# Counting passes tied to matmuls, tests moved into layer 1, and an earlier hub step in a two-layer graph kernel

## The chip, the cores and the metric

The kernel runs on one core of one Trainium2 chip. A core has a matmul engine (TensorE, PE in the profile, with its weight loads as PEld), a vector engine (VectorE, DVE), a scalar engine (ScalarE, ACT), GpSimd (POOL), a queue that issues plain transfers (SyncE, SP), and 16 DMA engines that serve the queues. The metric is the device time of one execution in microseconds (us), as the median of several runs.

## The reference

Two layers work on x of 2708 rows and 1024 columns, with a 2708 x 2708 matrix adj of zeros and ones, all float32.

```
layer 0:  q = x Wq^T + bq;  k = x Wk^T + bk;  v = x Wv^T + bv
          z = (q k^T / 32) * adj, where z == 0 becomes -10000
          x1 = layernorm(x + relu(softmax(z) v))
layer 1:  out = layernorm(x1 + adj (x1 W) + b)
```

adj is sparse: the chance of a one falls off with the square root of both the row's and the column's number, so that a few "hub" rows have many ones and most have few.

## The kernel before, in words

The kernel makes use of the sparseness. For each row it lists the columns that hold a one, sorts the rows by how many they have, and then gathers only the listed rows of x. Rows are worked on in 22 blocks of 128. A dense version of the whole computation stands behind it, and runs only if a flag is raised at the end: when a row has more ones than its block has slots, or when a score would make the shortcut wrong. Layer 1's output is already written by then; the flag is read last.

The stages, in the order of time:

1. **Product of M.** Since q k^T = x (Wq^T Wk) x^T, the weights are multiplied once into M (`product_of_m`, L739), as 28 half products of four steps each (`half_products`, L295; a float32 step appears as two matmuls in the profile). Alongside, rows of adj are loaded into three buffers in turn (`load_adj`), and `list_columns` (L230) lists a block: six range searches on DVE (L237), a counting pass on ACT over the same buffer (L240, a sign with a running sum), and some small DVE operations. Fourteen lists are called from here, one after every second half product. In the kernel before, the counting pass is part of `list_columns`, and an explicit dependency (`follow`) puts it behind the fourth search. It ends by asking for the next block's rows, which can be loaded when both the searches and the count are through with the buffer.
2. **y pairs.** y = x M + a constant row `y_bc` is what a row's scores are taken with. The first eight blocks (`FAMILY`) are made in four pairs (`y_pair`), each of seven half products. Before each of the first two pairs four more lists are called. Two sorts put the rows in order, one for the first eight blocks and one for the others (`sort_begin` makes classes on DVE, `sort_end` takes two small products of them on PE, at L664 and L668, and turns them into positions), and `records_out` writes the records in that order through POOL.
3. **y blocks.** The other 14 blocks of y (`y_block`, L377, 32 matmuls each). Beside them run the first attention jobs: `attend` gathers the y rows and the x rows of a block of sorted rows, takes the scores (L988), and sums x with the shares (L1045). `gather_onto` first copies `y_bc` into the buffer on ACT (L468) and then gathers y onto it with an adding transfer on POOL (L461).
4. **Layer 0's pairs.** Ten pairs of blocks, turned on PE (L907) and multiplied by Wv, then finished: bias, relu, residual, layernorm, and a scatter of x1 to memory (L894). In the last three pairs `row_constants` gathers rows of x (POOL) and multiplies each with a constant row on DVE (L1244).
5. **Layer 1.** Ten units of two blocks: gather and sum rows of x1 (`sum_rows`, L1412 and L1415), turn them, multiply by W, add the residual, layernorm, write. `test_scores` (L1255) runs ahead of it: it corrects the scores with the row constants, forms the tests, adds them over the partitions with a small product on PE (L1295), and sets the flag (L1296).

The most heavily filled rows are split over four partitions each, the "hub". `deal_hub` (L495) deals their columns out. It is a Python generator of ten steps, each called by a `next(deal)` at a chosen place. The fourth step computes places and the number `row` (L567 to L599), the fifth transposes `row` on PE (L602), the sixth to ninth gather the record and the eleven keys on POOL, and the tenth makes masks.

**What sets the order.** Each engine works through its own list in order. The lists are made when the program is built, by a scheduler that goes by priority (the order of the Python calls, and 2000 places ahead under `tc.high_priority(URGENT)`) and by its own estimate of when an operation's inputs are there. So an operation can stand earlier or later than its call: L1281 of `test_scores` runs at 319 us. `follow(later, earlier)` adds a dependency by hand, and with `same=True` one of order alone. `between[n]` holds things to be called after the n-th half product. A job list with estimated costs (`STEP`, `COST`, `credit`) decides after which step an attention job is called.

Of the kernel before, what the change touches and what calls it, by code (L numbers as in the profile page):

```python
# [9 lines left out]
F32 = mybir.dt.float32  # L10
# [11 lines left out]
P = 128  # L22
# [7 lines left out]
FAMILY = 8  # L30
# [51 lines left out]
def sparse_part(ctx, tc, x, xT, adj, wqT, wkT, wvT, bq, bk, bv, w1, b1, out):  # L82
# [28 lines left out]
    with es:  # L111
# [113 lines left out]
                    load_rows(a[:, cuts[i] + 8 * i:cuts[i + 1] + 8 * i], adj[:, cuts[i]:cuts[i + 1]], b * P, rows[b])  # L225
                loaded.append(a)

        listed = [0]

        def list_columns():  # L230
            b = listed[0]
            listed[0] += 1
            n, a = rows[b], loaded[b]

            at = lists.tile([P, RANGES, 8], U16, name="at_a", bufs=2)
            for i in range(RANGES):
                put = nc.vector.max_index(at[:n, i], ones[:n, :8], a[:n, cuts[i] + 8 * i:cuts[i + 1] + 8 * i + 8])  # L237
                if i == RANGES // 2:
                    behind = put
            put = nc.scalar.activation(junk[:n], a[:n, :AW].bitcast(U32), AF.Sign, accum_out=cnt[:n, b:b + 1])  # L240
            follow(put, behind)
            there = lists.tile([P, RANGES, 8], F32, name="there", bufs=2)
            nc.vector.tensor_tensor(there[:n], at[:n], ends[:n], op=ALU.is_lt)
            few = lists.tile([P, 8 * RANGES], F32, name="few", bufs=2)
            few3 = few.rearrange("p (i k) -> p i k", k=8)
            nc.vector.tensor_tensor(few3[:n], at[:n], base[:n], op=ALU.add)
            nc.vector.tensor_tensor(few3[:n], few3[:n], there[:n], op=ALU.mult)
            for i in range(0, KEYS, 8):
                nc.vector.max(keys[:n, b, i:i + 8], few[:n])
                if i + 8 < KEYS:  # L250
                    nc.vector.match_replace(few[:n], keys[:n, b, i:i + 8], few[:n], 0.0)
            load_adj()

        b_bc = a_bufs[2]
# [209 lines left out]
                follow(put, behind)  # L464
            return dst

        def gather_onto(what, src, at, n, dst):
            nc.scalar.copy(dst[:n], what[:n])  # L468
            return gather_at(src, at, n, dst, ALU.add)

        def gather_slot(src, at, n, dst):
# [267 lines left out]
        def product_of_m(acc, a, w, start, stop):  # L739
            nonlocal done, worked  # L740
            put = half_products(acc, a, w, start, stop)
            worked += 1
            while done < EARLY * worked // (7 * DC // 2):
                list_columns()
                done += 1
                if done == FAMILY + 1:
                    sort_begin(0)
            if not sorted_ and done > FAMILY + 2 and worked > 7 * DC // 2 - 4:
                sorted_.append(sort_end(0, put))
# [83 lines left out]

        wv_q = [None, quarters_of("wv", (1,))[0]]
        sorted_late = []
        for b in range(0, FAMILY, 2):
            while done < min(NB, EARLY + 4 * (b // 2 + 1)):
                list_columns()
                done += 1
            first = len(began)  # L840
            if b == 4:
                between[first + 6] = [lambda put: sorted_late.append(sort_end(1, put))]
            if b == 6:
                between[first + 5] = [lambda put: next(deal)]
            y_pair(b)
            if b == 0:
                records_out(*sorted_[0], 0, FAMILY, began[first + 1])
                records_back(0)
            if b == 2:
                load_last()  # L850
                sort_begin(1)
                bcast_rows(y_bc, y_col)
            if b in (0, 2):
                next(deal)
            if b >= 4:
                load_wv(range(DC // 2 + b - 4, DC // 2 + b - 2))
            if b == 4:
                records_out(*sorted_late[0], 0, NB - FAMILY)
# [28 lines left out]
            return gather_at(src, tabs[:rows[b], b, ROW:ROW + 1], rows[b], xr)  # L887

        def gather_y(b):
            return gather_onto(y_bc, y_ds[b >= FAMILY][:, :], tabs[:rows[b], b, OFF:OFF + 1], rows[b],  # L890
                               wp.tile([P, D], F32, name="yg"))

        def scatter(dst, b, n, src, group):
# [195 lines left out]
        def attend_shares(b, got):  # L1089
# [4 lines left out]
            else:  # L1094
                J, tab, far_less, rec, to, far, top = J0, tab0, less0, tab0, to_0, far_0, top2[:, 1:2]
                r = r_tile(b)
            yg = gather_onto(y_bc, y_ds[0][:, :], rec[:, OFF:OFF + 1], P, wp.tile([P, D], F32, name="yg"))
            for i, (j0, j1) in enumerate(pieces(J)):
                m = j1 - j0
                xg = [gather_slot(x, tab[:, j:j + 1], P, g_tile()) for j in range(j0, j1)]  # L1100
# [145 lines left out]

        def single_scores(b):
            n = rows[b]
            yg = gather_onto(y_bc, y_ds[b >= FAMILY][:, :], tabs[:n, b, OFF:OFF + 1], n, g_tile())
            xg = gather(x, b, 0, n)  # L1250
            s = stat.tile([P, 1], F32, name="s1")
            score(yg, xg, s[:n], n)
            masked_scores(b, 0, s[:n], less[:n, b, 0:1])

        def test_scores():  # L1255
# [35 lines left out]
            nc.vector.tensor_scalar(top2, top2, 9000.0, None, op0=ALU.is_gt)  # L1291
            nc.vector.tensor_max(some, some, top2[:, 0:1])
            nc.vector.tensor_max(some, some, top2[:, 1:2])
            mm = p_tr.tile([P, 4, P], F32, name="tr")
            nc.tensor.matmul(mm[:, 0, :1], ones, some, start=True, stop=True)  # L1295
            nc.vector.tensor_scalar(flag, mm[:1, 0, :1], 0.0, None, op0=ALU.is_gt)  # L1296

        credit = 0
# [11 lines left out]
        for i, (kind, b) in enumerate(steps):  # L1310
# [27 lines left out]
            if not left_y:  # L1338
                turn(i)
            if kind == "y":  # L1340
                if FAMILY + 1 <= b < FAMILY + 8:
                    next(deal)
                if b == FAMILY + 11:
                    records_back(1)
                    nc.sync.dma_start(out=bias_bc, in_=bv.to_broadcast([P, D]))
                (y_last if b == NB - 1 else y_block)(b)
                if b < FAMILY + 2:
                    load_wv(range(2 * (b - FAMILY), 2 * (b - FAMILY) + 2))
                if b == FAMILY + 1:
                    column_sums(NB - 1)  # L1350
                left_y -= 1
# [5 lines left out]
            elif kind == "mean":  # L1357
                rT = g_tile()[:, :DC * HUB].rearrange("p (c n) -> p c n", n=HUB)
                nc.scalar.copy(rT, xbT.unsqueeze(2).to_broadcast([P, DC, HUB]))
                po = project_mean(rT, wv_q)  # L1360
                pending = [(finish0, b_, po, gather_x(x, b_, b_ == last[-1])) for b_ in last]
            else:
                for k, b_ in enumerate(b):
                    pair_x[b_] = gather_x(x, b_, k)
                pending = [(finish_pair, b, project_pair(b, *turned[b]))]
                if i == len(steps) - 3:
                    u_bc = wp.tile([P, D], F32, name="u_bc", tag="yg")
                    bcast_rows(u_bc, u_col)
                if i >= len(steps) - 3:
                    row_constants((6, 8, 9)[i - len(steps) + 3])  # L1370
                if i == len(steps) - 2:
                    for b_ in single:
                        single_scores(b_)
                if b == pairs[0]:
                    bcast_rows(xb_bc[0], xbT)
                    spread.append(b)
# [5 lines left out]
        for p in pending:  # L1382
            p[0](*p[1:])
        assert not jobs and not c_left
        test_scores()


        xb_pool.release()
        cp = tc.alloc_tile_pool(name="c", bufs=1, side="right", reuse_waits="tile")
# [82 lines left out]
        for i, unit in enumerate(units):  # L1472
# [9 lines left out]
            if i == 4:  # L1482
                sum_rows("hub")
            pending = list(zip(unit, *work1(unit, *turned1.pop(i), xrs.pop(i))))
            if i in (4, 6):
                b = last[i // 2 - 2]
                pending.append((b, gather_x1(b), None))
# [322 lines left out]
```

## Time and profile before

The median of three runs is 1071.39 us (1070.51 to 1073.70). One execution was profiled.

| | |
|---|---|
| time of the profiled execution | 1075.12 us |
| its span, first to last instruction | 1073.4 us |
| PE busy | 960.5 us (89%) |
| DVE busy | 836.1 us (78%) |
| ACT busy | 410.8 us (38%) |
| POOL busy | 558.3 us (52%) |
| mean granted PE clock | 0.954 of full |
| bytes moved | 229 MB, 214 GB/s on average |

In time: the product of M ends at about 140 us, the y pairs at 254, the y blocks at about 454, layer 0's pairs at 744, and layer 1 goes on from 773 to the end.

A busy share says how long an engine worked, not whether anything waited for it. A wait names the engine or transfer that released it last. "Idle before" is the time that an engine stood still just before an instruction. The ends of PE's matmuls are modelled.

### The profile page before, as it was taken

Reading aid. Unit: us, or ns where it says so; the run is one execution under the profiler, and the core shown is the slowest. Engines: PE = TensorE matmul, PEld = TensorE weight load, DVE = VectorE, ACT = ScalarE, POOL = GpSimd, SP = SyncE. Lnnn points to the kernel's source line nnn. Section 1 sums busy time; section 2 is a strip of 40 time slices with the busy share of each in tenths; the row PEclk is TensorE's granted clock in tenths of the full one; section 3 lists DMA queues with packets and bytes.
Section 4 is the critical chain, followed back from the end, with each engine's and each line's share of the span. In section 5 each row is a group of like instructions: output and inputs, shape, how many; then the busy total and the mean of one; then the engine's idle time right before and its main releaser. Section 6 shows DMA issues by size and latency. Waiting matters only on the chain.

```text
span 1073.4 us, 10477 instructions
## 1 busy us (share of the span) xinstructions
PE 960.5 (89%) x2697; PEld 451.2 (42%) x2697; DVE 836.1 (78%) x2045; ACT 410.8 (38%) x917; POOL 558.3 (52%) x456
## 2 busy tenths in 40 slices
PE   7979897999949999999998989996299899989894
PEld 6434333444424444445543444442144344445341
DVE  8999998950697798958999888567859787868532
ACT  4244355542353423516343434322213333353431
POOL 0431163134668776216675663236687887758420
PEclk9998899899979999999999999999599899999998
DMA  9567767347988697327467974359797699977641
GB/s 356 165 181 244 225 193 228 118 145 240 286 276 225 177 291 210 108 60 272 136 179 225 243 217 147 130 180 368 273 275 231 213 306 289 326 217 222 205 117 42
DMA packets 103182, 229.21 MB, mean 214 GB/s; under 512 B 19775, under 2 KB 47175, under 8 KB 103113
## 3 DMA queue, kind: packets, MB, share of 16 engines
q0 software_dynamic: 51408, 159.09, 48.6%
q1 hardware_dynamic: 51704, 69.36, 19.9%
q8 instruction: 23, 0.38, 0.1%
q14 instruction: 47, 0.38, 0.1%
HBM read 218.08 MB, written 33.64 MB: 235 GB/s over the span
## 4 chain that ended last, share of the span: by engine, by line
PE 45%; DVE 15%; issue 15%; DMA 13%; POOL 8%; ACT 2%; another core or an unknown queue 0%; SPq 0%; POOLq 0%; DVEq 0%
PE po L297 29%; PE po L377 13%; DVE at_a L237 3%; POOL g L473 3%; DMA g<-in_x_dram,tabs 3%; DMA g<-x_d,tabs 2%; DVE junkv L988 2%; DVE r L1045 2%; DMA yg<-y_d,tabs 1%; DMA xr<-x_d,tabs 1%; PE tr L297 1%; DMA a<-in_adj_dram 1%; DVE part L1415 1%; DMA g<-x_d,tab 1%; PE tr L907 1%
## 5 line engine op out<-in xcount | busy, mean ns | idle before, releaser
L377 PE MATMUL po<-m,xt 128*128 128x512 f32 x416 | 181.9, 599 | 0.0
L297 PE MATMUL po<-t,s_all 128*128 128x512 f32 x320 | 147.3, 603 | 9.9 <-DVE xr L319 4.2
L988 DVE SCALAR_TENSOR_TENSOR junkv<-yg,g 128x1024 uint8<-128x1024 f32 x96 | 117.2, 1220 | 45.8 <-DMA yg<-y_d,tabs 29.7
L473 POOL DMA_INDIRECT g<-in_x_dram,tabs x77 | 101.4, 1317 | 45.4 <-issue 14.0
L377 PEld LDWEIGHTS po<-m,xt 128*128 128x128 f32 x416 | 79.6, 192 | 99.2 <-issue 98.7
L1415 DVE SCALAR_TENSOR_TENSOR r<-g,valid,r 128x1024 f32<-128x1024 f32 x77 | 98.3, 1283 | 15.0 <-DMA g<-x_d,tabs 9.5
L297 PEld LDWEIGHTS po<-t,s_all 128*128 128x128 f32 x320 | 61.0, 193 | 90.8 <-issue 72.0
L473 POOL DMA_INDIRECT g<-x_d,tabs x66 | 79.4, 1204 | 27.2 <-issue 16.4
L237 DVE FIND_INDEX8 at_a<-ones,a 128x8 uint16<-128x83 f32 (+3 forms) x132 | 83.5, 635 | 0.0
L240 ACT ACTIVATE junk<-a 128x2756 uint8<-128x2756 uint32 (+1 forms) x22 | 55.0, 2500 | 68.2 <-issue 36.4
L950 ACT ACTIVATE junks<-t,lnm 128x1024 uint8<-128x1024 f32 (+1 forms) x40 | 46.0, 1149 | 85.0 <-DVE lnm L948 83.9
L297 PE MATMUL po<-w,rT 128*128 128x512 f32 x160 | 74.3, 606 | 3.7 <-DVE t L1452 3.7
L297 PE MATMUL po<-wv,s_all 128*128 128x512 f32 x160 | 73.9, 606 | 3.0 <-DVE t L319 3.0
L1045 DVE SCALAR_TENSOR_TENSOR r<-g,pr,r 128x1024 f32<-128x1024 f32 x58 | 73.5, 1279 | 3.4 <-ACT r L1043 3.3
L297 PE MATMUL po<-wv,rT 128*128 128x512 f32 x160 | 74.4, 616 | 0.0
L297 PE MATMUL po<-t,rT 128*128 128x512 f32 x160 | 73.4, 601 | 0.5 <-DVE t L319 0.5
L297 PE MATMUL po<-w,s_all 128*128 128x512 f32 x160 | 72.3, 592 | 0.0
L963 ACT ACTIVATE t<-t,nmr,rstd 128x1024 f32<-128x1024 f32 (+1 forms) x40 | 49.1, 1238 | 59.3 <-DVE nmr L962 48.2
L908 ACT COPY rT<-tr 128x512 f32<-128x512 f32 x76 | 41.2, 589 | 78.3 <-PE tr L907 74.3
L450 ACT ACTIVATE junka<-xt 128x128 f32<-128x128 f32 x168 | 51.7, 308 | 41.8 <-PE po L297 21.9
L461 POOL DMA_INDIRECT xr<-in_x_dram,tabs x22 | 27.1, 1230 | 64.8 <-DVE t L1186 32.0
L1425 ACT COPY xr<-bias 128x1024 f32<-128x1024 f32 (+1 forms) x22 | 22.8, 1045 | 76.7 <-DVE t L1452 52.0
(414 smaller groups left out, 1742.9 us busy)
## 6 DMA issues: line engine op xcount, KB each, us to landing
xt<-in_xT_dram SPq DMA_DIRECT2D x21, 512.0 KB
y_d<-yo SPq DMA_DIRECT2D x21, 512.0 KB
a<-in_adj_dram SPq DMA_DIRECT2D x21, 413.5 KB
a<-in_adj_dram SPq DMA_DIRECT2D x21, 338.5 KB
a<-in_adj_dram SPq DMA_DIRECT2D x21, 263.5 KB
wq_i<-in_wqT_dram SPq DMA_DIRECT2D x8, 512.0 KB
wk_i<-in_wkT_dram SPq DMA_DIRECT2D x8, 512.0 KB
wv<-in_wvT_dram SPq DMA_DIRECT2D x16, 256.0 KB
```

The costliest lines, as they stand in the source:

```text
L237: put = nc.vector.max_index(at[:n, i], ones[:n, :8], a[:n, cuts[i] + 8 * i:cuts[i + 1] + 8 * i + 8])
L240: put = nc.scalar.activation(junk[:n], a[:n, :AW].bitcast(U32), AF.Sign, accum_out=cnt[:n, b:b + 1])
L297: put = nc.tensor.matmul(acc, a[:, k], w[:, k], start=start and k == 0, stop=stop and k == DC // 2 - 1, skip_group_check=True)
L377: put = nc.tensor.matmul(po, xts[b][:, c, :], m_q[c // 4][h][:, c % 4], start=(c == 0), stop=(c == DC - 1))
L450: put = nc.scalar.activation(junka[:, :xt.shape[2]], xt[:, c, :], AF.Copy, accum_out=xs[:, c, b:b + 1])
L473: nc.gpsimd.indirect_dma_start(out=dst[:n], out_offset=None, in_=src, in_offset=bass.IndirectOffsetOnAxis(ap=at, axis=0), bounds_check=N - ...
L908: nc.scalar.copy(rT[:, g * 4:g * 4 + 4, :], tr)
L950: nc.scalar.activation(junks[:n], t[:n], AF.Square, bias=nm[:n], accum_out=vs[:n])
L963: applied.append(nc.scalar.activation(t[:n], t[:n], AF.Identity, bias=nmr[:n], scale=rstd[:n]))
L988: nc.vector.scalar_tensor_tensor(junkv[:n], yg[:n], scale, xg[:n], op0=ALU.mult, op1=ALU.mult, accum_out=s)
L1045: nc.vector.scalar_tensor_tensor(r[:n], xg[j][:n], pr[:n, j:j + 1], r[:n], op0=ALU.mult, op1=ALU.add)
L1415: put = nc.vector.scalar_tensor_tensor(r[:n], xg[:n], ok[:n, j:j + 1], r[:n], op0=ALU.mult, op1=ALU.add)
```

## The change

- The counting pass leaves `list_columns` and becomes `count_columns(behind)`, which follows the half product handed to it. In the product of M a block that has been listed is counted after the next half product. In each of the first two y pairs two lists come before the pair and two after its second and fourth half products, and the counts after the first, third, fifth and seventh. The next load of adj is asked for in `count_columns`.
- `gather_onto` gets the block's number; for blocks 6 and 5 (`FIRST`) the copy of `y_bc` has the high priority.
- The hub's fourth step is called after the last y pair, and the later ones one y block earlier each.
- The four chunks of Wv that were loaded at the first two y blocks (two 256 KB halves each) are loaded one at a time at the fourth to seventh.
- The 23 row constants are taken 9, 9 and 5 in the last three pairs, before 6, 8 and 9.
- `test_scores` is called after the work of layer 1's seventh unit, and its last product and the flag (`raise_flag`) after that of the ninth, with an order behind PE's last product.

```diff
+        listed, counted = [0], [0]
 ...
-                put = nc.vector.max_index(at[:n, i], ones[:n, :8], a[:n, cuts[i] + 8 * i:cuts[i + 1] + 8 * i + 8])
-                if i == RANGES // 2:
-                    behind = put
-            put = nc.scalar.activation(junk[:n], a[:n, :AW].bitcast(U32), AF.Sign, accum_out=cnt[:n, b:b + 1])
-            follow(put, behind)
+                nc.vector.max_index(at[:n, i], ones[:n, :8], a[:n, cuts[i] + 8 * i:cuts[i + 1] + 8 * i + 8])
 ...
+        def count_columns(behind):
+            b = counted[0]
+            counted[0] += 1
+            n = rows[b]
+            put = nc.scalar.activation(junk[:n], loaded[b][:n, :AW].bitcast(U32), AF.Sign, accum_out=cnt[:n, b:b + 1])
+            follow(put, behind)
             load_adj()
 ...
-        def gather_onto(what, src, at, n, dst):
-            nc.scalar.copy(dst[:n], what[:n])
+        def gather_onto(b, what, src, at, n, dst):
+            if b in FIRST:
+                with tc.high_priority(URGENT):
+                    nc.scalar.copy(dst[:n], what[:n])
+            else:
+                nc.scalar.copy(dst[:n], what[:n])
             return gather_at(src, at, n, dst, ALU.add)
 ...
             worked += 1
+            if counted[0] < done:
+                count_columns(put)
             while done < EARLY * worked // (7 * DC // 2):
                 list_columns()
 ...
+        while counted[0] < done:
+            count_columns(began[-1])
         for b in range(0, FAMILY, 2):
-            while done < min(NB, EARLY + 4 * (b // 2 + 1)):
+            first = len(began)
+            if done < NB:
                 list_columns()
-                done += 1
-            first = len(began)
+                list_columns()
+                done += 4
+                for k in (1, 3, 5, 7):
+                    between[first + k] = [count_columns]
+                for k in (2, 4):
+                    between[first + k] = [lambda put: list_columns()]
 ...
-            if b in (0, 2):
+            if b in (0, 2, 6):
                 next(deal)
 ...
+            return some
+
+        def raise_flag(some):
             mm = p_tr.tile([P, 4, P], F32, name="tr")
-            nc.tensor.matmul(mm[:, 0, :1], ones, some, start=True, stop=True)
+            follow(nc.tensor.matmul(mm[:, 0, :1], ones, some, start=True, stop=True), products[-1], same=True)
             nc.vector.tensor_scalar(flag, mm[:1, 0, :1], 0.0, None, op0=ALU.is_gt)
 ...
-                if FAMILY + 1 <= b < FAMILY + 8:
+                if FAMILY + 1 <= b < FAMILY + 7:
                     next(deal)
 ...
-                if b < FAMILY + 2:
-                    load_wv(range(2 * (b - FAMILY), 2 * (b - FAMILY) + 2))
+                if 3 <= b - FAMILY < 7:
+                    load_wv([b - FAMILY - 3])
 ...
-                    row_constants((6, 8, 9)[i - len(steps) + 3])
+                    row_constants((9, 9, 5)[i - len(steps) + 3])
 ...
-        test_scores()
 ...
             pending = list(zip(unit, *work1(unit, *turned1.pop(i), xrs.pop(i))))
+            if i == len(units) - 4:
+                some = test_scores()
+            if i == len(units) - 2:
+                raise_flag(some)
```

## The prediction

> **What bounds the kernel now.** I read the page first: TensorE (PE) is busy 89% of the span, VectorE (DVE) 78%, and the chain that ended last is 45% PE. So the kernel is a row of matmuls with gaps, and the question is what ends each gap. The view of PE's waits answers it (columns: total us, times, longest us):
>
> ```profile
> PE tr L1295 <- DVE some L1293: 27.1, 1, 27.1
> PE tr L602 <- DVE scores L995: 13.7, 1, 13.7
> PE tr L297 <- ACT m L780: 11.3, 2, 7.9
> PE po L297 <- ACT yo L317: 7.8, 2, 6.7
> ```
>
> Each has one part of the change aimed at it. Then I read the timeline around each gap (start us, us, engine, line, operation, [idle before <- releaser]). First ScalarE (ACT) and PE at 74 to 91 us:
>
> ```profile
> 74.06 2.50 ACT L240 ACTIVATE junk<-a 128x2756 uint8<-128x2756 uint32 x1 [6.91 <-issue]
> 76.56 0.56 ACT L773 COPY m<-po 128x512 f32<-128x512 f32 x1
> 78.27 2.50 ACT L240 ACTIVATE junk<-a 128x2756 uint8<-128x2756 uint32 x1 [1.15 <-issue]
> 80.77 1.05 ACT L780 COPY m<-tr 128x512 f32<-128x512 f32 x2
> ...
> 81.48 10.05 PE L297 MATMUL tr<-wk_o,s_b 128*128 128x512 f32 x16 [7.86 <-ACT m L780]
> 91.36 7.03 PE L297 MATMUL po<-wk_o,s_a 128*128 128x512 f32 x16
> ```
>
> The counting pass L240 starts just as DVE's fourth range search ends (74.0, 78.1), and the copies that free PE's banks stand behind it. DVE itself has no gap from 33 to 87 us. It comes up with the second sort's classes only here, and PE uses them 8 us later:
>
> ```profile
> 213.97 1.54 DVE L658 TENSOR_SCALAR hot<-kk 128x14 f32<-128x14 f32 x19
> ...
> 223.36 0.61 PE L664 MATMUL tr<-hot,lower 128*128 128x266 f32 x2
> ```
>
> The hub's step: DVE stands still for the first y rows, then computes `row` between the scores, and PE's transpose waits for it:
>
> ```profile
> 273.78 1.22 DVE L988 SCALAR_TENSOR_TENSOR junkv<-yg,g 128x1024 uint8<-128x1024 f32 x1 [21.70 <-DMA yg<-y_d,tabs]
> ...
> 314.61 0.15 DVE L596 TENSOR_SCALAR row<-row 128x1 f32<-128x1 f32 x1
> ...
> 314.90 0.45 PE L602 MATMUL tr<-ident,row 128*128 128x128 f32 x1 [13.67 <-DVE scores L995]
> ```
>
> The layer switch, GpSimd (POOL), DVE and PE:
>
> ```profile
> 759.94 0.96 POOL L894 DMA_INDIRECT x_d<-t,tabs  x1 [0.30 <-ACT xr L1425]
> 767.44 1.03 POOL L473 DMA_INDIRECT g<-x_d,tabs  x1 [6.53 <-DMA x_d<-t,tabs]
> ...
> 772.45 0.73 DVE L1412 TENSOR_SCALAR r<-g,valid 128x1024 f32<-128x1024 f32 x1
> ...
> 773.33 1.94 PE L907 MATMUL tr<-ident,r 128*128 128x128 f32 x8 [0.99 <-DVE r L1412]
> ...
> 787.67 3.70 PE L297 MATMUL po<-t,s_all 128*128 128x512 f32 x8 [0.70 <-DVE xr L319]
> ```
>
> The 27 us are put down to the flag, but layer 1 can't gather before the last scatter of x1 lands at 767.2. So most of that gap has another owner.
>
> **What the Trainium skill says.** "Perfetto Trace Analysis", Tensor Engine Instruction: ACT, DVE and GpSimd run strictly in order. The trace agrees: an ACT copy with its input ready stands behind L240. "TensorE: Matmul & The Clock Gate", Part 1: an idle stretch of some 3.4 us halves PE's clock until a busy stretch of that length restores it. Here 16 matmuls after the 7.86 us wait took 10.05 us, the next 16 took 7.03: a wait costs 3.0 us more than itself.
>
> **The change part by part.** Times are against the profiled run, 1075.12 us, span 1073.4 and 1.7 around it; it is 3.7 us (0.35%) above the median of the runs, 1071.39.
>
> *A, counting passes.* Nothing is removed: 22 passes of 2.5 us stay on ACT, but they wait for a finished product, not for DVE. In the product of M list j follows product 2j and its count product 2j+1, so a count of 2.7 us comes ahead of that product's copy (0.6) while the next product takes 3.43 (8 x 0.43): 3.3 against 3.43, no wait. In the y pairs the yo copies have the high priority and go first. Behind a count stand ACT's copies and column sums, and for the copies PE; since the count waits only for a product that PE has passed, I cost the new wait at 0. If the cover is gone, it is 0.2 us at four products. The next row load is issued after the count, as before behind both readers of the buffer; DVE is the later of the two, so loads don't move. Two of four lists in each of the first y pairs move behind products: same DVE work.
>
> What PE can gain: ahead of L664 it waits 7.86 + 3.45 + 1.90 + 1.07 + 6.68 = 21.0, and the slow clock adds 3.0 + 3.0 (8 matmuls at 112.31 took 6.57, not 3.60) + 1.75 (at 189.83, 5.35, not 3.60) = 7.75. Alone it would be at L664 at 223.4 - 28.7 = 194.7. But DVE is late next. Its idle time from 20 us to the classes is 4.3 (record gather) + 2.8 + 2.0 + 0.8 (for PE), 9.9 in all; without it the classes are done at 215.5 - 9.9 = 205.6. So PE stands at 206 rather than 223.4, 17.4 gained, and PE's new waits for DVE (11 us in some pieces: first sort, differences t3 and t4, second sort) cost one slow clock of 3.0. Take 14.4; low 8 if DVE keeps half its idle time and PE pays more slow clocks; high 22 if the order puts the sort later on PE.
>
> *D, hub step.* Step four's DVE work, 11 x 0.34 (L586) and some 16 x 0.16, 6.3 us, moves into DVE's 21.7 us idle before 273.8, so `row` is ready before the scores start. PE's 13.67 go. Issued one y block earlier with it: the record and eleven key gathers on POOL, about 1.2 + 0.3 each, ahead of x gathers; a DVE wait of 6.1 follows them at 330 now and moves with them. Of the 13.67, DVE catches up only 6.3 of its own; the other 7.4 eat its lead. It has one: from 457 to 500 it waits 7.3 + 6.3 for PE. But at 577.8 PE waits 2.99 for a row sum, so I give 4 back: 9.7. Low 4 (the lead is gone by block 12), high 13.7.
>
> *y rows' fill and value weights.* The two copies of y_bc run now at 236.6 and 237.9, their gathers at 266.9: they are early already, so 0 for the priority. Unless it puts them ahead of yo copies (rival 3). Eight weight loads of 256 KB leave 255.8 to 281.7, where the DMA engines are 93 to 100% busy; 2 MB at 300 GB/s are 7 us of transfers less before the scores. "DMA: Bandwidth & Descriptors", SWDGE vs HWDGE vs iDMA, says that an engine serves its queues in turn, so the gathers share with them; the 6.9 us of the gather at 266.92 fit that. It helps DVE by perhaps 3 us, not PE: 0. They are needed at block 19 and come by block 15.
>
> *G, layer switch.* Row constants go from 6, 8, 9 to 9, 9, 5: at the end 4 gathers fewer, 4 x 1.26 = 5.0 us of POOL, 4 x 1.3 = 5.2 of DVE, 2 MB (6.4 us at 329 GB/s). Now the last gather ends at 757.8, the scatters follow at 758.1 and 759.9; the second t is ready at 757.9, its small operations held by two row constants (1.6 and 2.0 us). So the last scatter comes between 758.2 and 754.3, and lands in 6.3 us or, with less queued ahead of it, about 4: layer 1 begins 2 to 8 us sooner, take 5. The tests (767.0 to 771.6 on DVE, some 5 us) leave the path of r. "DMA: Bandwidth & Descriptors", Anatomy of one DMA, gives 2.0 us + bytes/436 GB/s; an estimate for 512 KB is 3.2, so the first gather lands at 770.6 and r gains 1.8. But PE then stands at 787.67 for xr, which POOL issues after eight other gathers: 0 of it stays. In layer 1 tests cost DVE 5 us at the seventh unit, where DVE is busy 38.5 of 57 us (960 to 1017): 0, or 2 if uncovered. The flag's product waits for nothing two units later. The 4 constants moved ahead put 1.3 us each on DVE and a gather each in the third and second last pairs, where PE already waits 1.34 and 2.07 behind them: minus 1 (0 to 3).
>
> Sum: 14.4 + 9.7 + 5 - 1 = 28.1. Profiled 1047.0, median 1071.4 - 28.1 = 1043.
>
> **The rivals.** *1, handed back:* DVE is the bound and PE's gaps only move. For: DVE has no idle in 40 to 80 and 120 to 160, and the hub's gain is not DVE's. Against: PE waits 8.3 us for DVE in all from 457 to 744. A 8, D 4, G 2, minus 2: 12 gained, 1059. *2, all of it:* the planned order defers the sorts, and A 22, D 13.7, G 8 come: 43, 1028. Against: DVE's 20 us stretches without idle. *3, slower:* the two urgent y_bc fills reach ACT's queue right after y_bc (203.6 now) while their buffer still holds sorting data, which POOL reads until 247.5. ACT then stands, the next pair's yo copies behind it, and PE after one product more. Up to 44 us, slower from 28 on; at 34, 1077. Against: now they wait 0.24. *4, nothing:* the scheduler keeps the counts behind the searches anyway; little speaks for it.
>
> **How the numbers follow.** Forecast 0.60 (1033 to 1052), rival 1 0.21 (1052 to 1065), rival 2 0.10, rival 3 0.06, rival 4 0.03. The likeliest is 1043; low 1030 and high 1060 leave out half of rival 2, the far part of rival 1, and 3 and 4, about 0.18. A measurement tells 0.3% (3.2 us) from no change: faster 0.91, same 0.03, slower 0.06.
>
> **What would show it.** Right: no PE wait for an ACT copy before 140 us; new PE waits for DVE (hot, y_t) there; L664 near 206; no wait at L602; the gap at the switch still some 20 us, owned by r and not by the flag; first layer-1 gather some 29 us sooner. Wrong: PE waiting for ACT yo copies behind yg fills, or row-sum waits of over 5 us from 440 to 740.

## The result, and the profile after

The changed kernel is slower: 1077.11 us median of 20 runs (1069.91 to 1083.67), against 1073.42 us for the kernel before, measured beside it in 20 runs. The ratio is 1.0037, with a 95% interval of 1.0015 to 1.0059. Forecast was a ratio near 0.974. Single executions lie up to 0.7% from their median, so the times below are told as such ratios. A profile is one execution, and is read for what waits on what.

PE's waits in the changed kernel (total us, times, longest us; here and below, `...` stands where lines are left out):

```profile
PE tr L923 <- DVE r L1429: 25.1, 1, 25.1
PE po L380 <- ACT yo L320: 16.7, 7, 5.2
PE po L300 <- DVE yo L322: 11.0, 2, 10.1
...
PE po L431 <- ACT yo L320: 6.4, 1, 6.4
PE po L300 <- DVE m L322: 4.0, 1, 4.0
```

All four waits shown of before are gone: the two for ACT's copies ahead of the y blocks (11.3 and 7.8), the 13.7 for the hub's row, and the flag's. In their place stand new ones: for ACT's copies *inside* the y blocks (L380 and, for the last row block, L431), where before had none, and for DVE before them.

The counting pass now comes after a product, and PE runs through (timeline of ACT, then of PE; times as in the views of before):

```profile
71.00 2.50 ACT L253 ACTIVATE junk<-a 128x2756 uint8<-128x2756 uint32 x1 [2.90 <-PE tr L300]
...
74.38 0.59 ACT L789 COPY m<-tr 128x512 f32<-128x512 f32 x1 [0.32 <-PE tr L300]
```

```profile
67.32 7.03 PE L300 MATMUL tr<-wk_o,s_a 128*128 128x512 f32 x16
74.21 7.11 PE L300 MATMUL tr<-wk_o,s_b 128*128 128x512 f32 x16
```

The second sort's product, 223.36 before, comes at 217.76, behind three new waits for DVE (PE's timeline):

```profile
120.65 10.04 PE L300 MATMUL po<-wk_o,wq_o 128*128 128x512 f32 x16 [4.00 <-DVE m L322]
...
162.52 5.85 PE L300 MATMUL po<-y_t,xt 128*128 128x512 f32 x8 [10.06 <-DVE yo L322]
...
217.76 0.98 PE L671 MATMUL tr<-hot,lower 128*128 128x266 f32 x2 [1.78 <-DVE hot L665]
```

The y blocks then start at 247.65 (before: 254.27), and the hub's transpose no longer waits (it stood 13.67 us before):

```profile
261.47 0.27 PE L609 MATMUL tr<-ident,row 128*128 128x128 f32 x1
```

At this point PE is 6.6 + 13.7 = 20.3 us ahead of the kernel before. It then loses all of it, and more:

```profile
311.74 14.00 PE L380 MATMUL po<-m,xt 128*128 128x512 f32 x32 [1.93 <-ACT yo L320]
...
372.11 15.46 PE L380 MATMUL po<-m,xt 128*128 128x512 f32 x32 [3.15 <-ACT yo L320]
391.27 15.70 PE L380 MATMUL po<-m,xt 128*128 128x512 f32 x32 [3.70 <-ACT yo L320]
...
436.60 5.28 PE L431 MATMUL po<-m,x_last 128*32 128x256 f32 x64 [6.38 <-ACT yo L320]
```

The y blocks end at 461.88, where they ended at 453.63 before: 8.25 us later. The books balance: 20.3 ahead, less 16.7 + 6.4 = 23.1 of waits, leaves some 5.4 us, which PE's slow clock after the longer waits accounts for (the products of the last row block took 5.28 us, and 3.66 before).

Why does ACT hold PE? ACT works strictly in order (the Trainium skill says so in "Perfetto Trace Analysis", Tensor Engine Instruction, and this trace agrees). Its list mixes three things: copies of y blocks (into `yo`, L320) out of PE's four banks, the buffers in which a product stands until it is copied; fills of `yg` (L475); and exponents of the attention (L1040, L1131). The last two wait for DVE: a fill for the scores that still read its buffer, an exponent for the maximum (`nm`) of its scores. ACT's timeline:

```profile
310.15 1.05 ACT L475 COPY yg<-y_bc 128x1024 f32<-128x1024 f32 x1 [9.45 <-DVE junkv L1004]
311.11 0.58 ACT L320 COPY yo<-po 128x512 f32<-128x512 f32 x1
...
328.81 0.30 ACT L1040 ACTIVATE pr<-scores,nm 128x4 f32<-128x4 f32 x1 [9.20 <-DVE nm L1031]
329.24 1.15 ACT L1059 ACTIVATE r<-g,pr 128x1024 f32<-128x1024 f32 x1
330.29 0.56 ACT L320 COPY yo<-po 128x512 f32<-128x512 f32 x1
```

The exponent at 328.81 stands 9.2 us for a maximum on DVE, the y copy behind it with it, and PE resumes at 330.91 after 5.17 us. A half of a y block takes PE 6.9 us, so with four banks it can be three halves, 20.6 us, ahead of ACT's copies. From 311 us on it is: the copy at 311.11 is of a half whose product had ended some 22 us earlier (the sixth; the tenth starts at 311.74 in its bank). And DVE is late because its scores wait for gathers (`tabs` is the table of the listed columns). DVE's waits from 266 to 420 us, before and then after:

```profile
DVE junkv L988 <- DMA yg<-y_d,tabs: 25.5, 3, 21.7
DVE junkv L988 <- DMA g<-in_x_dram,tabs: 8.1, 3, 6.1
```

```profile
DVE junkv L1004 <- DMA yg<-y_d,tabs: 17.9, 2, 16.3
DVE junkv L1004 <- DMA g<-in_x_dram,tabs: 17.4, 9, 4.3
```

The wait for x rows has doubled, and comes nine times in place of three. From DVE's first score to the same maximum further on, before takes 273.78 to 413.19 (139.4 us) and after 270.05 to 414.16 (144.1), although 6.3 us of row arithmetic have left this stretch.

These waits take PE's lead, and one more makes the loss. PE turns the maxima of the hub's rows (L1130, now L1146) at 422.04 before and at 422.22 after, so it is level there. Of the 8.25 us, 8.0 come behind that point: the wait of 6.38 us for the last row block and 1.62 us of slow clock after it. PE waits there for ACT's 21st copy of a half. In before this copy stands ahead of an exponent in ACT's list, after it stands behind it (ACT's timeline, before and then after):

```profile
419.73 0.57 ACT L317 COPY yo<-po 128x512 f32<-128x512 f32 x1
...
432.91 0.30 ACT L1115 ACTIVATE pr<-scores,nm 128x5 f32<-128x5 f32 x1 [11.88 <-DVE nm L1109]
```

```profile
435.69 0.30 ACT L1131 ACTIVATE pr<-scores,nm 128x5 f32<-128x5 f32 x1 [13.70 <-DVE nm L1125]
...
435.99 0.56 ACT L320 COPY yo<-po 128x512 f32<-128x512 f32 x1
```

So ACT's planned order has changed as well. No run moves this copy alone, so what it costs by itself is not shown.

At the layer switch the gap is owned by `r`, not by the flag:

```profile
766.93 1.19 POOL L910 DMA_INDIRECT x_d<-t,tabs  x1 [5.52 <-ACT t L997]
770.74 1.04 POOL L480 DMA_INDIRECT g<-x_d,tabs  x1 [2.61 <-DMA x_d<-t,tabs]
```

```profile
776.32 1.94 PE L923 MATMUL tr<-ident,r 128*128 128x128 f32 x8 [25.05 <-DVE r L1429]
```

From PE's last product of layer 0 to its first of `r` it was 28.7 us (744.6 to 773.33), now 25.1. Of the 8.25 us by which the y blocks end later, layer 0's pairs give back 1.6, this gap 3.6 and layer 1 2.2, so the two profiled executions end 0.8 us apart. The medians are 3.7 us apart.

### The profile page after: what moved, and what is told of

Its sections match the earlier page's. It is cut to its first block, busy times and chain, and to the rows that moved or that the text cites. A ratio compares the mean times of both kernels' runs of the same rounds, so it can differ in the third digit from the quotient of the medians.

```text
span 1074.2 us, 10455 instructions
## 1 busy us (share of the span) xinstructions
PE 961.5 (90%) x2697; PEld 452.7 (42%) x2697; DVE 835.9 (78%) x2045; ACT 410.1 (38%) x917; POOL 556.5 (52%) x456
## 4 chain that ended last, share of the span: by engine, by line
PE 31%; DVE 19%; issue 19%; DMA 17%; POOL 11%; ACT 1%; SPq 0%; POOLq 0%; DVEq 0%; ACTq 0%
PE po L300 26%; DVE at_a L237 5%; POOL g L480 5%; DMA g<-x_d,tabs 3%; DMA g<-in_x_dram,tabs 3%; DMA xr<-x_d,tabs 2%; PE po L380 2%; DVE junkv L1004 2%; POOL xr L464 2%; PE tr L923 2%; POOL yg L464 1%; DMA a<-in_adj_dram 1%; DMA xr<-in_x_dram,tabs 1%; DVE r L1061 1%; PE po L431 1%
## 5 line engine op out<-in xcount | busy, mean ns | idle before, releaser
L380 PE MATMUL po<-m,xt 128*128 128x512 f32 x416 | 186.1, 607 | 16.7 <-ACT yo L320 16.7
L380 PEld LDWEIGHTS po<-m,xt 128*128 128x128 f32 x416 | 80.0, 195 | 120.1 <-issue 96.1
L480 POOL DMA_INDIRECT g<-in_x_dram,tabs x77 | 94.5, 1227 | 48.2 <-issue 14.0
L480 POOL DMA_INDIRECT g<-x_d,tabs x66 | 76.9, 1165 | 22.4 <-issue 16.5
L923 PE MATMUL tr<-ident,r 128*128 128x128 f32 x304 | 41.8, 288 | 31.3 <-DVE r L1429 25.1
```

Source lines behind the costliest of these rows:

```text
L380: put = nc.tensor.matmul(po, xts[b][:, c, :], m_q[c // 4][h][:, c % 4], start=(c == 0), stop=(c == DC - 1))
L480: nc.gpsimd.indirect_dma_start(out=dst[:n], out_offset=None, in_=src, in_offset=bass.IndirectOffsetOnAxis(ap=at, axis=0), bounds_check=N - ...
L923: nc.tensor.transpose(tr[:, k, :], r[:, c * P:(c + 1) * P], ident)
```

## The experiments

All ratios are to the kernel before, run beside the kernel in question, with 95% intervals. The names "order", "copies" and "gathers" are used below for the three suspects: DVE's planned order of scores and sums (theory C in the expectations); y copies held in ACT's list (theory B); the hub's key gathers on POOL (theory A).

### Which part costs

`a_only`: the counting passes alone (`count_columns`, its calls, and the new loop over the y pairs).

> The kernel before with the counting passes tied to products, and nothing else of the change. Theory (the attention loop of the y phase, DVE's scores and the gathers, sets when the y blocks can end, and ACT's queue hands that to PE): the second sort's product comes some 5 us sooner, the wait of 13.7 us for the hub's row (L602) stays or shrinks, and nothing or next to nothing is left at the turn after the last y block; time within 0.3% of before (1068 to 1076 against a before of 1072). Rival (the new order on DVE, the hub's search ahead of the second sort's classes, is itself the loss): over 0.3% slower, 1076 to 1080. The prediction's own step: 14 us faster, 1058.

Measured: 0.9916 (0.9889 to 0.9943), 9.0 us faster. The second sort's product came at 216.36 and the y blocks started at 245.88, 8.4 us sooner than before; the wait at the hub's row was 15.5 us. My expectation that nothing would be left was wrong: sooner y rows let the first score start sooner (267.62 in place of 273.78), so the whole attention loop moved (the same maximum at 407.31 in place of 413.19).

`d_only`: the hub's steps one turn sooner, alone.

```
-            if b in (0, 2):
+            if b in (0, 2, 6):
                 next(deal)
...
-                if FAMILY + 1 <= b < FAMILY + 8:
+                if FAMILY + 1 <= b < FAMILY + 7:
                     next(deal)
```

> The kernel before with the hub's steps one turn sooner, and nothing else. Theory (the y phase is bound by the attention loop, and the hub's twelve gathers on POOL now stand ahead of the first x gathers): PE's 13.7 us wait goes, but comes back as waits of PE for ACT's copies of the y blocks, and the last y block ends no sooner, perhaps later; 0 to 0.7% slower, 1072 to 1080. Rival (the hub's step is worth its wait once PE doesn't also come 14 us sooner): faster by some 5 to 10 us, 1062 to 1067.

Measured: 1.0111 (1.0064 to 1.0158), 12 us slower. This alone shows all that was seen in the changed kernel: the 13.7 us are gone, and come back as copies (PE's waits, then DVE's from 266 to 420 us):

```profile
PE po L377 <- ACT yo L317: 17.8, 7, 5.8
...
PE po L428 <- ACT yo L317: 6.5, 1, 6.5
```

```profile
DVE junkv L988 <- DMA g<-in_x_dram,tabs: 19.9, 11, 4.8
```

`g_only`: row constants 9, 9, 5 and the moved tests and flag, alone.

> The kernel before with the layer switch's parts (row constants 9, 9, 5; tests and flag's product in layer 1), and nothing else. Theory: the gap at the switch shrinks by 3 to 4 us, as in the whole change, and nothing is handed back, since nothing before the last pairs is touched: 1067 to 1070, 0.2 to 0.4% faster. Rival (tests in layer 1, or the constants moved into earlier pairs, cost what the gap gives): within 0.1% of before.

Measured: 0.9982 (0.9956 to 1.0008), a gain of 1.9 us that the interval doesn't tell from none. In its profile the gap was 24.82 us.

`no_hub`: the whole change with the two lines of `d_only` put back.

> The whole change but for the hub's steps, which stay where they were before. Theory (the sooner hub step is what turns the other parts' gain into a loss): 0.3 to 1% faster than before, 1061 to 1069, with PE waiting some 10 to 18 us at the hub's row again and few us for ACT's copies after it. Rival (the y phase ends when the attention loop lets it, whatever the hub does): the wait at the hub's row is back and the y phase ends where it did before, time within 0.4% of before, some 1068 to 1073, owed to the layer switch alone.

Measured: 0.9898 (0.985 to 0.9946). PE waits again for the hub's row, and not for copies:

```profile
PE tr L609 <- DVE scores L1011: 11.3, 1, 11.3
```

So the hub's sooner step is what turns a gain of 1.0% into a loss of 0.4%. The parts multiply: 0.9916 x 0.9982 = 0.9898, which leaves nothing for the y rows' fill and the value weights, though each factor is known to some 0.3 to 0.5% only. With the 1.0111 the product is 1.0008 for the whole, against 1.0037 measured; the intervals don't tell these apart.

### Gathers, copies or order?

`keys_late`: the whole change, but the record and key gathers stay at their old blocks.

```
-                if FAMILY + 1 <= b < FAMILY + 7:
+                if FAMILY + 1 <= b < FAMILY + 8 and b != FAMILY + 2:
```

> The whole change, but the record and key gathers of the hub on POOL keep the places among the y blocks that they had before; the row's arithmetic and its transpose stay one block sooner. Theory A (the sooner key gathers, ahead of the x gathers that DVE's scores wait for, are what costs): the first partial row maximum on DVE comes some 7 us sooner than in the whole change, PE's waits for ACT's copies shrink from 23 us to under 12, and the time is 1% below before or better (1060 to 1066 against 1074). Theory B (PE's head start over the attention loop is what is handed back, through ACT's queue, wherever the gathers stand): PE still waits 15 us or more for ACT's copies, the y blocks end within 4 us of where they do in the whole change, and the time stays within 0.5% of before.

Measured: 1.0033 (1.0015 to 1.005), as the whole change. The first partial maximum came 4.7 us sooner (323.95), but PE still waited 14.1 + 5.8 us for copies. So the gathers' place makes no difference that these runs show.

`spare`: the second half of each y block in one of the three banks of the transposes.

```
             for h in range(NH):
-                po = bank()
+                po = spare_bank() if h else bank()
```

> The whole change, and the second half of each y block goes into one of the three PSUM banks that serve the transposes: up to seven banks stand between a product and ACT's copy, in place of four. Theory B (ACT's queue, in which a copy stands behind exponents and fills that wait for DVE, holds PE): four banks are 14 us of products, of which 7 to 10 are used up by one such stall; three more banks cover it, PE's waits for ACT's copies in the y blocks fall from 23 us to under 8, the y blocks end 12 to 20 us sooner, and the time is 1056 to 1064, 1 to 1.6% faster than before. Rival (the attention loop sets the end of the y phase by itself): PE's waits only move to the turn after the y blocks, where it waits for row sums: within 0.4% of the whole change.

Measured: 0.9982 (0.9962 to 1.0001), 0.55% better than the whole change, half of what was expected. (The 14 us of that expectation were too few: a half takes 6.9 us, not 3.5.) PE's timeline shows why. It ran without a wait from 246 to 397 us, then met the attention itself:

```profile
390.43 7.03 PE L380 MATMUL tr<-m,xt 128*128 128x512 f32 x16
411.14 0.48 PE L1146 MATMUL tr<-ident,nm 128*128 128x128 f32 x1 [13.68 <-ACT yo L320]
```

The transpose at 411.14 turns a maximum that DVE had only at 410.04. (The releaser named is ACT's copy at 410.52 out of the transposes' banks, which stands in ACT's list behind the exponent that waits for this maximum.) Later PE waited 5.11 us for `den`, a sum of the attention. As I read it, copies are the door through which PE is held, and the attention loop decides when it opens.

`spare_keys_late`: both edits.

> Both of the two edits before: the key gathers at their old places and the second half of each y block in a spare bank. If both theories hold, the y blocks end where PE's own work puts them, some 20 us sooner than in the whole change, and the time is 1050 to 1058. If the attention loop bounds the y phase, it is no better than the better of the two single edits (within 0.3%).

Measured: 0.9989 (0.9961 to 1.0016): no better than the banks alone.

`no_hub_spare`: the banks, with the hub's step where it was.

> The change without the hub's sooner step, and the second half of each y block in a spare bank. Theory B: there PE comes late anyway, since it waits 11 us at the hub's row, and its waits for ACT's copies after that are few; so the spare banks give nothing or up to 4 us: 1064 to 1070. Rival (the spare banks help in themselves): as much faster as they make the whole change.

Measured: 0.9961 (0.994 to 0.9982), 0.6% slower than `no_hub` (0.985 to 0.9946), where the intervals barely overlap. Neither theory had that the banks cost something there. With them, the sooner hub step costs 0.2% (0.9982 to 0.9961) in place of 1.4%.

That left the order. The attention takes a block's gathered rows in pieces of three to six. From the traces, DVE's first five pieces in its list, with S a score, R a weighted sum, a dot one operation of the row arithmetic (128 x 128) and | the maximum of a piece:

```
before      SSSS|SSSRSR|SSS.RSR.R|.S..SR.R.R.R.S.S.SSS|SSSRSR|
after       ...........SSSS|SSSRSR|SSSSRSR|SRSSSRRSRSR|SSRSRSR|
sums_first  ...........SSSS|SSRRSS|SSRRRSSS|SSRRRRSSSS|SSRRRRRSS|
filler      ...........SSSS|SS.RSRS|.S.S.RSRSR.|S..SR.R.R.R.SSSSS|SSSR|
```

A sum takes x rows that its score has read before, so they have landed, and it sets their buffers free for the next gathers; a score waits for a gather. In the fourth piece of before, four sums stand right behind the second score. After, two stand behind the fourth score, one behind the fifth, one behind the sixth: DVE, which works in order, stands at a score (1.20, 2.06 and 3.20 us at the third, fourth and fifth) while the sums behind it hold the buffers that later gathers need. This is read from the lists; the next runs test it. Taking eleven small operations from among the scores had made the builder plan the rest in another order.

`sums_first`: the whole change, and in the y phase an order within DVE alone.

```
                 for j in range(m):
-                    score(yg, xg[j], s[:n, j:j + 1], n)
+                    put = score(yg, xg[j], s[:n, j:j + 1], n)
+                    if j >= 3 and summed and left_y:
+                        follow(put, summed[-1], same=True)
```

(`summed` holds the last sum of each piece; `score` returns its instruction. Asked for were the fourth and later scores; in the list printed above the third stands behind the sums too.)

> The whole change, and in the y phase the fourth and later scores of a piece stand behind the weighted sums of the piece before in DVE's order (no wait on another engine is added). Theory C (with the hub's row arithmetic gone from among the scores, the planned order puts weighted sums, which free gather buffers, behind scores that wait for a gather; the loop of gathers grows by some 10 us): the maxima on DVE come 5 to 10 us sooner than in the whole change, DVE's waits for gathers between the first score and 414 us shrink by as much, and the time is 0.5 to 1.2% below the whole change (0.992 to 0.999 of before). Theory B alone (PE's head start is handed back through ACT's queue whatever DVE's order): within 0.3% of the whole change, 1.001 to 1.007 of before.

Measured: 0.9939 (0.9921 to 0.9957), 1.0% better than the whole change. DVE's waits for x rows of `tabs` fell from 17.4 us to 3.1, the maximum at 414.16 came at 404.60, and PE's waits for copies in the y blocks fell to 5.6 us:

```profile
DVE junkv L1004 <- DMA g<-in_x_dram,tabs: 3.1, 4, 1.2
```

But ACT's list changed with DVE's: the 21st copy stands ahead of the exponent again (410.42 and 426.46), and the wait at the last row block is gone. So the gain of "order", here and in `d_sums` further on (418.98 and 436.11), is that of both lists.

`filler`: the whole change, plus eleven operations of the row arithmetic's size, results unused, tied by `follow` to the last product before the second y block.

```
+                if b == FAMILY + 1:
+                    fill_dve()
                 (y_last if b == NB - 1 else y_block)(b)
```

> The whole change, plus eleven operations on DVE of the size of the hub's row arithmetic (128 x 128, 0.34 us each, results unused), tied to the last product before the second y block, so that DVE's planned order has such work among the first scores again while PE doesn't wait for it: 3.7 us of work added. Theory C: the order of the next pieces is again one with sums ahead of scores, so in spite of the added work it is faster than the whole change, 0.995 to 1.001 of before. Theory B: as the whole change or slower, 1.003 to 1.008 of before.

Measured: 0.9992 (0.9967 to 1.0017): 0.45% faster than without the added work, with four sums right behind the second score of the fourth piece, as in before. The waits for x rows were 9.3 us. Here the 21st copy still stands behind the exponent (433.02 and 432.72), and PE waits 9.7 us at the last row block. So this run has DVE's order without ACT's, and gains less than `sums_first`, with 3.7 us of added work in it.

`before_sums` and `d_sums`: the same order in the kernel before, and in that of `d_only`.

> The kernel before, with DVE's order forced in the y phase (fourth and later scores of a piece behind the weighted sums of the piece before), nothing of the change. Theory C (the forced order only mends what the sooner hub step spoils): within 0.3% of before. If the forced order speeds up the loop in itself, 0.990 to 0.996, and the gain of the run with the sums first says little on the hub step.

> The kernel before, with the hub's steps one turn sooner and DVE's order forced. Theory C (the order is what the hub step's loss of 1.1% consists of): the loss goes, 0.997 to 1.004 of before. Rival (the hub step also loses by its gathers on POOL and by PE's head start going through ACT's queue): some 0.5% or more of the loss stays, 1.005 to 1.011.

Measured: 0.9969 (0.9949 to 0.9988) and 1.0024 (0.9997 to 1.0051). Neither expectation held whole: the order is worth 0.3% in itself, and 0.9% where the hub's step is sooner. With it, that step still costs 0.55% (1.0024 against 0.9969) in place of 1.1%. So in the kernel before, order is about half of the loss, though the intervals leave this open by a third either way.

`no_hub_sums_first`: the order, without the sooner hub step.

> The change without the hub's sooner step, and DVE's order forced as in the run with the sums first. Theory C: there the order was good already, so the forced one gives nothing or little: 0.985 to 0.993 of before. If forcing in itself speeds the loop, 0.980 or less; if the forced order is worse than the planned one, 0.995 or more.

Measured: 0.9908 (0.9873 to 0.9944), no different from `no_hub`. Against `sums_first` (0.9939), the sooner hub step costs 0.3% when the order is forced, in place of 1.4%: in the changed kernel order is rather three quarters of the loss, with the same reserve.

`sums_spare`: whole change, order and banks.

> The whole change, DVE's order forced, and the second half of each y block in a spare bank. If both causes (order, and ACT's copies that hold PE) add up: 0.984 to 0.990 of before, better than any run so far. If the loop of scores and gathers alone sets the end of the y phase, the banks give nothing more: 0.992 to 0.996.

Measured: 0.9915 (0.989 to 0.9939), which the intervals don't tell from the order alone (0.9939). PE waited 14.0 us in one piece for `den` of the shares (L1161): again the attention.

### The second sort

`search_late`: `no_hub`, with the hub's search on DVE called later, inside the third y pair.

> The change without the hub's sooner step, and the hub's search (four times the eight largest, on DVE) behind the second sort's classes in place of ahead of them. Theory (the search, which the counts' new places put ahead of the classes, is why the second sort's product came 5.6 us sooner and not 17.4): that product comes at 206 to 212 us in place of 218. In the end little of it stays, since the first scores wait for y rows and not for the sort: 0.986 to 0.993 of before. Rival (DVE is full until then in either order): the product stays at 216 to 219 us.

Measured: 0.9909 (0.9878 to 0.994), product at 217.88. DVE's list kept the search among the classes, so this run says nothing on the question.

`search_behind`: `no_hub`, with the search tied behind the classes within DVE.

```
             follow(put, products[-1])
+            follow(put, hot_put[0], same=True)
```

> The change without the hub's sooner step, and on DVE the hub's search (ten times the eight largest and what takes them out, some 16 us) placed behind the second sort's classes by an order within DVE alone. The run with the search called later left DVE's order as it was, so it said nothing on this. Theory (the search among the classes is what kept the second sort's product at 218 us): the product comes at 203 to 209 us, as the prediction had it. As to time: 0.985 to 0.991 of before if the sooner sort also brings the gathers sooner, 0.991 to 0.995 if the search, now later, holds up the hub.

Measured: 0.9905 (0.9876 to 0.9935). The product came without any wait for DVE, but at 213.25, not at 206. Against 217.88 in `search_late`, the search was worth some 4.6 us of that product's place. The rest is PE's own: it had waited 10.1 us for DVE's `yo` and 4.0 for `m`, and came no sooner. Next to nothing of the 4.6 us is left: right after the product PE waits 2.86 us for DVE's `yo`, and the half product after that starts at 222.41, against 223.06.

### A better version

Six kernels lie between 0.9898 and 0.9916 and can't be told apart. `no_hub`, the change without its two lines on the hub, is 1.0% faster than before. `a_only`, the counting passes alone, gives 0.8% with still less of the change.

## Why the prediction was wrong

**A, counting passes: right in kind, too large.** Predicted 14.4 us, measured alone 9.0 (6.1 to 12.0 from the interval), near its low end of 8. The five waits for ACT went as said. The term that was mis-sized is "DVE is late next ... PE stands at 206": it stands at 217.8 (216.4 alone). Its waits for DVE add up to 17.9 us, not 11 (10.06, 4.00, 1.78 and three of under 1 us), and two of them brought slow clocks of 3.0 and 2.2 us where one of 3.0 was allowed. That is the way from the prediction's 194.7 to 217.8. Of the product's place, some 4.6 us were the hub's search among the classes. I had counted DVE's idle time, and not what DVE would do first: while PE waits the 10.06 us for `yo`, DVE works through the range searches of the next lists (150.9 to 161.8), and the copy that PE needs stands behind them.

**D, hub step: wrong in sign. This is the step that failed.** Predicted 9.7 us gained; measured alone 12 lost. The sentence at fault is "PE's 13.67 go ... the other 7.4 eat its lead. It has one". I looked for DVE's lead in the stage after (457 to 500), and not within the y phase, where PE depends on DVE at every y block through ACT's list: with four banks PE can be 20.6 us ahead of ACT's copies, and ACT's copies keep DVE's time. In before PE never waited for ACT in this phase, but ACT for PE (11.2 us in seven waits ahead of column sums); 20.3 us sooner, PE met the limit. So PE's wait at the hub's row was slack against the attention loop. What a step frees on PE there is lost at the next copy, with slow clocks on top. And "6.3 us, moves into DVE's 21.7 us idle" took the other operations' order as fixed; the plan around them changed on DVE and on ACT, and the scores' waits for x rows grew by 9 us. What the runs show of the split is this: a forced order takes the step's cost from 1.1% to 0.55% in the kernel before and from 1.4% to 0.3% in the changed one, and seven banks in place of four take it from 1.4% to 0.2%. Either removes most of the 1.4%, so order and copies look like two links of one chain and not like two shares of a sum; but the banks changed other things too, and the exact split stays open. The place of the eleven key gathers, which I had named as a cost, made no difference that the runs show (1.0033 against 1.0037).

**y rows' fill and value weights: 0, not contradicted.** The product of the parts leaves nothing for them, to within some 0.5%; neither was run alone. The urgent fills ran at 231.77 without blocking ACT.

**G, layer switch: owner right, size smaller.** The gap is owned by `r`, as said, and shrank by 3.6 us of the 5 less 1 predicted. Alone the part measured 1.9 us, between a loss of 0.9 and a gain of 4.7. The place of the gain was partly wrong: the last scatter comes no sooner after PE's last product (15.7 us; 15.3 before), but after it POOL waits 2.61 us for the landing and no longer 6.53, where I had put 4 for 6.3. The tests on DVE didn't leave the switch: they run from 769.9 to 774.6 (before: from 767.0 to 771.6), and DVE still waits 0.65 us for `r`'s rows after them.

**The rivals.** Rival 3 named the very sign that came ("PE waiting for ACT yo copies behind yg fills", at 1077), but for a wrong reason: not the urgent fills, but the ordinary ones and the exponents, which had always stood there (for the fills ACT waited 44.2 us before and 53.5 after, for the exponents 42 and 55), and which PE had been too late to meet. That its 1077 is the measured median is luck. Rival 1, "handed back", was right for D and far too small: it kept 4 us.

## What to carry to other kernels

A wait on the engine that bounds the kernel is worth its length only if the loop beside it isn't due just after. Before removing one, follow the next few buffers that the engine needs (here four banks emptied by an in-order engine) to whoever empties them, and ask how far ahead it may run. Taking small operations out of a planned order can change the order of the large ones: compare the two lists, of every engine on the way, and pin the order that sets buffers free.

## What was not expected of the hardware

- Added work made the kernel faster: eleven unused DVE operations, 3.7 us, gave 0.45% (`filler`). This is the order of the lists, not the chip, but only a trace shows it.
- PE's slow clock cost less in the y blocks than the 3.0 us that I had taken for each wait, and the cost doesn't follow the wait's length. After waits of 3.15 and 3.70 us, 32 matmuls took 15.46 and 15.70 us in place of 14.0, some 1.5 to 1.7 more; after a wait of 1.93 us, nothing. After the wait of 4.00 at 120.65 it was 3.0. But a wait of 3.36 us at 851.20 cost nothing (8 matmuls in 3.70 us), and one of 2.07 us at 732.26 in before cost 1.8 (8 in 5.40). The Trainium skill ("TensorE: Matmul & The Clock Gate", Part 1) tells of a free-running window of some 3.4 us. A price that varies from wait to wait fits that, and a single price, as I took it, doesn't. That a wait of 2.07 us, shorter than such a window, was followed by a slow clock, the page doesn't explain; here the measurement stands.
